# ReLU on VectorE, and forty gathered columns a turn in place of thirty-six

## The chip, the core and the metric

The kernel runs on one core of one Trainium2 chip. The core has TensorE (PE in the profile, its weight loads PEld), VectorE (DVE), ScalarE (ACT), GpSimd (POOL) and SyncE (SP). Each engine has an instruction queue of its own, worked off in order; rows of the profile marked with a q (DVEq, ACTq) are instructions that the queue's sequencer does itself, such as loading registers, and they don't count as busy. The metric is device time in microseconds of one execution, as the median of several runs. The span of a profile is the time from the first to the last instruction of one execution.

## The reference: what is computed

One layer of a graph network with 12,500 nodes of 64 features and 212,500 directed edges, sorted by their destination, with 32 features each:

```python
msg_in = jnp.concatenate([nodes[row], nodes[col], edge_features], axis=-1)
messages = _mlp(msg_in, mW1, mb1, mW2, mb2)      # relu(x @ W1 + b1) @ W2 + b2, hidden size 128
aggregated = jax.ops.segment_sum(messages, col, num_segments=nodes.shape[0])
upd_in = jnp.concatenate([nodes, aggregated], axis=-1)
return _mlp(upd_in, uW1, ub1, uW2, ub2)
# outside: x = _layernorm(x + this)
```

`row` is the source and `col` the destination of an edge. The source's features have to be fetched edge by edge, since sources are in no order; destinations come in order, so the edges of a stretch concern few neighbouring nodes.

## The kernel before, in words

Edges are worked on in groups of 384 (three tiles of 128); there are 554 groups, and the main loop of `ordered` (L718) has one turn for each. A turn of TensorE, written by `step` (L677), is three pieces of work for three different groups, with a single completion signal behind the last of them:

- `turn(k)` (L423): three transposes bring the gathered source features and a one-hot of the destinations (together 96 columns) of group k into PSUM (L429). ScalarE copies the result into the block `own_st` in SBUF (L440).
- `hidden(k - 2)` (L448): three matmuls with the weights `own_wm` (L453) give the hidden layer before the ReLU in PSUM. ScalarE makes the ReLU, 128x384, into `own_h` (L464).
- `sums(k - 4)` (L474): matmuls add the hidden rows by destination (L481) and count them (L486). VectorE adds both to the sums on the chip, at an address taken from a register (L495 and L496).

The next turn but one needs the same PSUM banks again, so TensorE may be one turn ahead of ScalarE and VectorE.

Source features arrive in one of two ways. For most groups GpSimd gathers rows of `x` from HBM by indirect DMA, three per group (L184), 16 groups ahead of the turn, into a ring of 20 buffers; a gather waits until the group 20 before has been copied out of its buffer and until that turn's copies on ScalarE are done (`marks_by`). For the groups listed in `COPIED` nothing is gathered: the transposed features of all nodes lie in SBUF (`own_xc`, 64 partitions by 12,500 nodes), and VectorE (L599) and ScalarE (L601) copy one column, 64 partitions by 4 bytes, per edge from there into `own_st`. `COLS` is how many columns are copied in each turn, from turn 18 (`BEGIN`) to turn 543. A group of 384 columns is listed as soon as the copies so far, `COLS` a turn, have filled it (L89 to L91); with `COLS` of 36 the list has 49 groups, the last of them 541. `VCOLS = (12, 8)` are VectorE's portions in a turn and `ACOLS = (16,)` ScalarE's.

A copy's source address comes from a register. `registers(k, part)` (L565) loads the addresses of one portion into registers of the engine (L578, TENSOR_LOAD on the engine's queue, as many registers as the portion has columns); `fetch(part)` (L585) issues the copies. The addresses themselves come by a DMA for eight turns at once (L557) and are scaled by one operation of VectorE (L563). `places` (L366, load at L371) loads four addresses for the additions, every fourth turn.

The order of VectorE's queue in a turn is: load of 12 addresses, two additions (L495, L496), 12 copies, the one-hot of a group six turns on (L412), load of 8 addresses, 8 copies. That the load of 12 stands ahead of the additions, which wait for TensorE, is the work of the list `between` (L738, popped at L493). ScalarE's queue in a turn is: copy of the transposed group (L440), ReLU (L464), 16 copies with addresses loaded in the turn before, load of 16 addresses for the next turn (L771).

Into the turns, pieces of `update` (L500) are placed: as soon as all edges of a chunk of nodes are done, its second layer and normalisation are computed, in six steps of one per turn (L528 and L543 among VectorE's operations). The last ten turns (`SHORT`) copy nothing and use shorter steps.

Of the kernel before, what the change touches and what calls it, by code (L numbers as in the profile page):

```python
# [14 lines left out]
AF = mybir.ActivationFunctionType  # L15
ALU = mybir.AluOpType
# [16 lines left out]
G = (E + GE - 1) // GE  # L33
# [17 lines left out]
BEGIN = 18  # L51
CHECKED = 8
VCOLS = (12, 8)
ACOLS = (16,)
COLS = sum(VCOLS + ACOLS)
SPAN = 8
STREAMS = ()
# [4 lines left out]
def tiles_of(g):  # L62

    n = min(GE, E - g * GE)
    return [min(P, n - j * P) for j in range((n + P - 1) // P)]
# [27 lines left out]
for _, rate, _ in STREAMS:  # L93
    BY_ROWS.append([])
    while True:
        last = BEGIN + (P * (len(BY_ROWS[-1]) + 1) - 1) // rate + ROW_LEAD
# [33 lines left out]
def ordered(ctx: ExitStack, tc: tile.TileContext, a, own, ok):  # L130
# [3 lines left out]
    nc = tc.nc  # L134
# [18 lines left out]
    loads, places_by, copy_by, relu_by, sums_by, wm_by, turn_by = ({} for _ in range(7))  # L153
# [5 lines left out]
    def after(first, *others):  # L159

        tc.declare_no_dep(first.ins, group="quiet", reason="waits for the last of a step")
        for i in others:
            tc.add_manual_dep(
                first.ins, i.ins.name,
                mybir.DependencyInfo(mybir.DependencyClass.Sync, mybir.DependencyReason.DATA),
                reason="the kernel's own rings",
            )
        return first
# [73 lines left out]
    def bit(k):  # L242

        nodes = [NEAR_NODES + (N - NEAR_NODES) * i // BITS for i in (k, k + 1)]
        tiles = [first + (NT - first) * i // BITS for i in (k, k + 1)]
        nc.sync.dma_start(src_sb[:, slice(*tiles)], a["src"][:, slice(*tiles)])
        nc.sync.dma_start(xc[:D, slice(*nodes)], a["xT"][:, slice(*nodes)])
        rest(nodes[0], nodes[1] if k < BITS - 1 else NP)

    def zeroed(k):  # L250

        n0, n1 = (NP * i // BITS for i in (k, k + 1))
        nc.vector.memset(agg[:, n0:n1], 0.0)
# [108 lines left out]
    def columns(g):  # L362
        t, c = own.st[g // SB % BLOCKS], (g % SB) * GE
        return t, c, sum(tiles_of(g))
# [83 lines left out]
    def hidden(g, ps):  # L448
        t, c, n = columns(g)
        sizes = tiles_of(g)  # L450
        pre = ps[1][:, : TG * H].rearrange("p (j h) -> p j h", h=H)
        did = [
            nc.tensor.matmul(pre[:p, j, :], t[:, c + j * P : c + j * P + p], wm[g % NW],  # L453
                             start=True, stop=True)
            for j, p in enumerate(sizes)
        ]
        needs = [*copy_by[g], *columns_by.get(g, {}).values(), wm_by[g], efs_by[g // SB],
                 *(wm_loads[g] if g < NW else ())]

        def relu(step):  # L460
            hidden_by[g] = step
            h = own.h[g % NH]
            if len(set(sizes)) == 1:
                relu_by[g] = [nc.scalar.activation(h, pre, AF.Relu)]  # L464
            else:
                relu_by[g] = [nc.scalar.activation(h[:p, j, :], pre[:p, j, :], AF.Relu)
                              for j, p in enumerate(sizes)]
            for i in relu_by[g]:
                after(i, step, *([sums_by[g - NH]] if g >= NH else []))
            return relu_by[g]  # L470

        return did, needs, relu

    def sums(g, ps):  # L474
        h, s = own.h[g % NH], own.s[g % RING]
        sizes = tiles_of(g)
        sg = ps[2][:, : TIMES * W].rearrange("p (t w) -> p t w", w=W)
        counted = ps[2][0:1, TIMES * W :][:, :W]
        did = []
        for j, p in enumerate(sizes):  # L480
            did.append(nc.tensor.matmul(  # L481
                sg, h[:p, j, :],
                s[:p, j, D:].unsqueeze(1).to_broadcast([p, TIMES, W]),
                start=j == 0, stop=j == len(sizes) - 1))
        for j, p in enumerate(sizes):
            did.append(nc.tensor.matmul(counted, own.one[:p], s[:p, j, D:],  # L486
                                        start=j == 0, stop=j == len(sizes) - 1))

        def add(step):
            sums_by[g] = step  # L490
            at = bass.ds(starts.pop(g), W)
            count = xc[COUNT : COUNT + 1, at]
            if between:  # L493
                between.pop()()
            a = after(nc.vector.tensor_tensor(agg[:, at], sg[:, 0, :], agg[:, at], ALU.add), step)  # L495
            return [a, after(nc.vector.tensor_tensor(count, counted, count, ALU.add), step)]  # L496

        return did, [*relu_by[g], *copy_by[g]], add
# [60 lines left out]
    def addresses(i):  # L559

        if i in indices:
            t = indices[i][:, : min(SPAN * COLS, GE * len(COPIED) - i * SPAN * COLS)]
            nc.vector.tensor_scalar(t, t, 4.0, float(own.at), ALU.mult, ALU.add)  # L563

    def registers(k, *parts):  # L565

        i, n = divmod(k - BEGIN, SPAN)
        if i < 0:
            return
        all_parts = [*((ET.DVE, c) for c in VCOLS), *((ET.Activation, c) for c in ACOLS)]  # L570
        for part in parts:
            engine, count = all_parts[part]
            c0 = (k - BEGIN) * COLS + sum(c for _, c in all_parts[:part])
            count = min(count, GE * len(COPIED) - c0)
            if count <= 0:
                return
            b = c0 - i * SPAN * COLS
            _, v = nc.values_load_multi_w_load_instructions(  # L578
                indices[i][0:1, b : b + count], engines=[engine],
                min_val=own.at, max_val=own.at + 4 * (N - 1),  # L580
                skip_runtime_bounds_check_because="a source is one of the nodes",
            )
            held[part] = engine, c0, v
# [42 lines left out]
    def row_addresses(n, i):  # L626

        if (n, i) in row_index:
            t = row_index[n, i][:, : row_span(n, i)[1]]
            nc.vector.tensor_scalar(t, t, 4.0 * D, None, ALU.mult)  # L630
# [82 lines left out]
    for n in range(len(STREAMS)):  # L713
        row_indexes(n, 0)
    made = summed = 0
    between, held, last = [], {}, {}

    for k in range(G):  # L718
        if k < BITS:
            bit(k)  # L720
            if k + 2 < BITS:
                zeroed(k + 2)
        if 1 < k < len(TABLE):
            projected(k)
        if k == CHECKED:
            addresses(0)
            for n in range(len(STREAMS)):
                row_addresses(n, 0)
            combined()
            ordered_edges()  # L730
            early.close()
            up = ctx.enter_context(tc.tile_pool(name="upd", bufs=2))
        if k % SB == 2:
            inputs(k // SB + 2)
        if k % SB == 1:
            places(k // SB + 1)
        if k < G - SHORT:
            between.append(lambda: registers(k, 0))  # L738
            step((turn, k), *([(hidden, k - 2)] if k > 1 else []),
                 *([(sums, k - 4)] if k > 3 else []))  # L740
            made, summed = max(0, k - 1), max(0, k - 3)
            if between:
                between.pop()()
        else:

            step((turn, k))
            for _ in range(2):
                if summed < made:
                    step((sums, summed))
                    summed += 1  # L750
            for _ in range(2):
                if made <= k:
                    step((hidden, made))
                    made += 1
            registers(k, 0)
        fetch(0)
        window(k + SB)
        for n in range(len(STREAMS)):
            row_numbers(n, k)
            row_fetch(n)  # L760
        onehot(k + LEAD)
        marks_by[k] = [copy_by[k][-1]]
        if k < G - 1:
            for part in range(1, len(VCOLS + ACOLS)):
                if part != len(VCOLS):
                    registers(k, part)
                fetch(part)
                if part >= len(VCOLS) and ET.Activation in last:
                    marks_by[k].append(last[ET.Activation])
            if k + 1 < G - 1:  # L770
                registers(k + 1, len(VCOLS))  # L771
            if k >= BEGIN and (k - BEGIN) % SPAN == 0:
                indexes((k - BEGIN) // SPAN + 1)
            if k >= BEGIN and (k - BEGIN) % SPAN == SPAN - 2:
                addresses((k - BEGIN) // SPAN + 1)
        if k + AHEAD < G:
            gather(k + AHEAD)
# [333 lines left out]
```

## Time and profile before

| | |
|---|---|
| median of three runs | 1913.65 us (1913.47 to 1916.86) |
| the profiled execution's own time | 1914.16 us |
| its span | 1912.4 us |
| mean granted TensorE clock | 0.972 |
| busy: GpSimd, ScalarE, TensorE, VectorE | 1431.7, 1325.2, 1324.3, 1251.4 us |
| gathers (L184) | 1514 |
| copied columns on VectorE (L599) and ScalarE (L601) | 10,460 and 8,356 |
| register loads on VectorE and ScalarE (L578) | 1,046 and 523 |

In a row of the list of groups, the numbers behind the bar are busy time in us (overlapping instructions counted once) and the mean duration of one in ns; behind the second bar stands the engine's idle time just before these instructions and what ended most of it. A row of waits has the total in us, how often, and the longest. A row of a stretch has its limits, its length, the busy time with the count of instructions that overlap the stretch, then the granted clock, the DMA share and GB/s. A row of time order has the start, the length, the instruction, and in brackets the idle time before it. A row of one source line has the minimum, median and maximum duration in ns, and the first and last start in us. Copies on one engine overlap each other, so that their mean duration is longer than the time from one to the next.

### The profile page before, as it was taken

The page shows a single profiled execution, that of the slowest core. Times are in us where ns is not written, and L with a number is a line of the kernel's source. Part 1 is how long each engine was busy: PE and PEld are TensorE (multiplying, and loading weights), DVE is VectorE, ACT ScalarE, POOL GpSimd, SP SyncE. Part 2 cuts the span into 40 slices and gives each one's busy share as a digit, 9 for nine tenths or more (in the row PEclk, how much of TensorE's full clock was granted, in tenths as well). Part 3 has the DMA queues.
Part 4 walks back from the last instruction along what each step waited for, and adds up shares of the span by engine and source line. Part 5 has one row for each costly group of instructions (what it writes and reads, how often), then busy time and mean ns, then how long its engine had stood idle before and what let it go on. Part 6 is the DMA issues. An engine that isn't in the chain of part 4 may idle for free. (4 is left out here: it accounts for less than half of the span.)

```text
span 1912.4 us, 56586 instructions
## 1 busy us (share of the span) xinstructions
PE 1324.3 (69%) x12323; PEld 1170.6 (61%) x12323; DVE 1251.4 (65%) x12584; ACT 1325.2 (69%) x9559; POOL 1431.7 (75%) x1521
## 2 busy tenths in 40 slices
PE   5877777767767766676666776766766766667677
PEld 4766666666656655665655665655656655556566
DVE  4347777766666666676766766666667666676662
ACT  4468787766767767776767776776676677676662
POOL 7777777777777777777777777777777777777774
PEclk9889999989999999999999999999999999999998
DMA  5532222222222222222222212222222222222221
GB/s 141 139 97 64 53 50 52 49 49 48 45 53 52 46 52 48 49 49 48 53 48 48 50 44 53 52 46 52 48 50 48 51 47 52 45 53 48 49 50 25
DMA packets 113836, 105.15 MB, mean 55 GB/s; under 512 B 52115, under 2 KB 83488, under 8 KB 113488
## 3 DMA queue, kind: packets, MB, share of 16 engines
q0 software_dynamic: 48448, 49.68, 13.6%
q1 hardware_dynamic: 64196, 51.29, 9.7%
q8 instruction: 104, 1.70, 0.4%
q14 instruction: 244, 2.00, 0.3%
q10 hardware_dynamic: 844, 0.48, 0.1%
HBM read 91.68 MB, written 9.62 MB: 53 GB/s over the span
## 5 line engine op out<-in xcount | busy, mean ns | idle before, releaser
L184 POOL DMA_INDIRECT own_s<-in_x,src_sb x1514 | 1430.9, 945 | 462.5 <-issue 261.5
L599 DVE COPY own_st<-own_xc 64x4 uint8 x10460 | 896.5, 191 | 27.7 <-DMA by_dst<-t 3.5
L601 ACT ACTIVATE own_st<-own_xc 64x4 uint8 x8356 | 847.3, 195 | 2.9 <-DMA by_dst<-t 2.9
L429 PE MATMUL own_ps<-own_ident,own_s 128*96 128x128 f32 x1661 | 289.0, 284 | 540.4 <-DMA own_s<-in_x,src_sb 355.6
L440 ACT ACTIVATE own_st<-own_ps 96x384 f32<-96x384 f32 (+1 forms) x554 | 268.6, 485 | 506.7 <-PE own_ps L486 483.7
L429 PEld LDWEIGHTS own_ps<-own_ident,own_s 128*96 128x96 f32 x1661 | 164.3, 129 | 602.0 <-ACT own_h L464 445.0
L481 PE MATMUL own_ps<-own_s,own_h 128*128 128x128 f32 x3322 | 478.6, 282 | 1.3 <-ACT own_h L464 0.6
L495 DVE TENSOR_TENSOR own_agg<-own_ps,own_agg 128x32 f32 x554 | 106.3, 192 | 567.1 <-PE own_ps L486 386.4
L453 PE MATMUL own_ps<-own_wm,own_st 128*128 128x128 f32 x3322 | 476.5, 281 | 0.0
L481 PEld LDWEIGHTS own_ps<-own_s,own_h 128*128 128x128 f32 x3322 | 431.1, 198 | 2.8 <-ACT own_h L464 1.6
L453 PEld LDWEIGHTS own_ps<-own_wm,own_st 128*128 128x128 f32 x3322 | 428.6, 197 | 1.3 <-issue 0.5
L464 ACT ACTIVATE own_h<-own_ps 128x384 f32<-128x384 f32 x553 | 264.8, 479 | 21.2 <-PE own_ps L453 20.0
L486 PE MATMUL own_ps<-own_s,own_one 128*1 128x32 f32 x3322 | 189.1, 194 | 0.0
L486 PEld LDWEIGHTS own_ps<-own_s,own_one 128*1 128x1 f32 x3322 | 113.8, 83 | 69.4 <-issue 5.7
L412 DVE TENSOR_TENSOR own_s<-iota,dlc 128x96 f32<-128x96 f32 x554 | 137.3, 248 | 0.7
L496 DVE TENSOR_TENSOR own_xc<-own_ps,own_xc 1x32 f32 x554 | 102.1, 184 | 31.9 <-PE u_ps L507 13.2
L383 PE MATMUL u_ps<-w1b,own_xc 65*128 65x128 f32 x196 | 31.8, 310 | 32.0 <-DMA own_xc<-in_xT 12.7
L383 PEld LDWEIGHTS u_ps<-w1b,own_xc 65*128 65x128 f32 x196 | 26.8, 211 | 35.0 <-issue 20.3
L519 PE MATMUL u_ps<-same,own_xc 65*128 65x64 f32 (+1 forms) x196 | 39.5, 283 | 0.4 <-ACT u L512 0.4
L386 ACT ACTIVATE t<-u_ps 128x512 f32<-128x512 f32 (+1 forms) x25 | 14.7, 588 | 36.2 <-DMA by_dst<-t 20.0
L521 PE MATMUL u_ps<-u,u 128*128 128x64 f32 (+1 forms) x196 | 38.2, 277 | 0.0
L519 PEld LDWEIGHTS u_ps<-same,own_xc 65*128 65x128 f32 (+1 forms) x196 | 29.9, 192 | 2.5 <-ACT u L512 1.0
(60 smaller groups left out, 264.4 us busy)
## 6 DMA issues: line engine op xcount, KB each, us to landing
own_st<-in_efT SPq DMA_DIRECT2D x138, 192.0 KB
own_s<-in_x,src_sb POOLq DMA_INDIRECT x1514
own_wm<-by_dst SPq DMA_DIRECT2D x554, 16.0 KB
by_dst<-t SPq DMA_DIRECT2D x24, 256.0 KB
out<-o SPq DMA_DIRECT2D x24, 128.0 KB
own_xc<-in_xT SPq DMA_DIRECT2D x12, 179.2 KB
index<-in_src_copied SPq DMA_DIRECT2D x65, 1.1 KB
dlc_i<-in_dst_cols SPq DMA_DIRECT2D x1, 807.0 KB
```

The lines of the kernel that those rows point to most:

```text
L184: nc.gpsimd.indirect_dma_start(out=s[:p, j, :D], out_offset=None, in_=x[:, :], in_offset=bass.IndirectOffsetOnAxis(ap=src_sb[:p, g * TG + ...
L412: places_by[g] = nc.vector.tensor_tensor(own.s[g % RING][:, :, D:], iota.unsqueeze(1).to_broadcast([P, TG, W]), dlc[:, g * TG : (g + 1) * ...
L429: nc.tensor.transpose(xt[:, j * P : j * P + p], sides[g] if g in sides and j == TG - 1 else s[:p, j, :], ident[:p, :p])
L440: after(nc.scalar.activation(t[r, c : c + n], xt[r, :n], AF.Copy), step))]
L453: nc.tensor.matmul(pre[:p, j, :], t[:, c + j * P : c + j * P + p], wm[g % NW], start=True, stop=True)
L464: relu_by[g] = [nc.scalar.activation(h, pre, AF.Relu)]
L481: did.append(nc.tensor.matmul(sg, h[:p, j, :], s[:p, j, D:].unsqueeze(1).to_broadcast([p, TIMES, W]), start=j == 0, stop=j == len(sizes) - 1))
L486: did.append(nc.tensor.matmul(counted, own.one[:p], s[:p, j, D:], start=j == 0, stop=j == len(sizes) - 1))
L495: a = after(nc.vector.tensor_tensor(agg[:, at], sg[:, 0, :], agg[:, at], ALU.add), step)
L496: return [a, after(nc.vector.tensor_tensor(count, counted, count, ALU.add), step)]
L599: by[engine] = nc.vector.tensor_copy(o, x_at)
L601: by[engine] = nc.scalar.activation(o, x_at, AF.Copy)
```

## The change

Three things are changed together. The ReLU of a group is made by VectorE (`tensor_scalar` with max against 0) and not by ScalarE. `ACOLS` is (8, 4, 4, 4) in place of (16,), so ScalarE copies 20 columns a turn, each portion loaded into registers just before its copies, and `COLS` is 40. And the list `between` is gone: VectorE's load of 12 addresses stands behind the ReLU and the two additions, and ScalarE's first load (8 addresses) stands behind L440 in the same turn, no longer at the end of the turn before.

```diff
-ACOLS = (16,)
+ACOLS = (8, 4, 4, 4)
...
             if len(set(sizes)) == 1:
-                relu_by[g] = [nc.scalar.activation(h, pre, AF.Relu)]
+                relu_by[g] = [nc.vector.tensor_scalar(h, pre, 0.0, None, ALU.max)]
             else:
-                relu_by[g] = [nc.scalar.activation(h[:p, j, :], pre[:p, j, :], AF.Relu)
+                relu_by[g] = [nc.vector.tensor_scalar(h[:p, j, :], pre[:p, j, :], 0.0, None, ALU.max)
                               for j, p in enumerate(sizes)]
...
             count = xc[COUNT : COUNT + 1, at]
-            if between:
-                between.pop()()
             a = after(nc.vector.tensor_tensor(agg[:, at], sg[:, 0, :], agg[:, at], ALU.add), step)
...
         if k < G - SHORT:
-            between.append(lambda: registers(k, 0))
             step((turn, k), *([(hidden, k - 2)] if k > 1 else []),
                  *([(sums, k - 4)] if k > 3 else []))
             made, summed = max(0, k - 1), max(0, k - 3)
-            if between:
-                between.pop()()
...
-            registers(k, 0)
+        registers(k, 0)
+        if k < G - 1:
+            registers(k, len(VCOLS))
         fetch(0)
...
-            if k + 1 < G - 1:
-                registers(k + 1, len(VCOLS))
```

More of the change, by code (lines that the diff above doesn't have):

```diff
@@ L715, in ordered @@
     made = summed = 0
-    between, held, last = [], {}, {}
+    held, last = {}, {}
     for k in range(G):
```

## The prediction

> **What bounds the kernel now.** I read the page first, then who waits for whom, then the turns counted by stretch, and last single turns of VectorE in order of time.
>
> ```profile
> span 1912.4 us, 56586 instructions
> PE 1324.3 (69%) x12323; PEld 1170.6 (61%) x12323; DVE 1251.4 (65%) x12584; ACT 1325.2 (69%) x9559; POOL 1431.7 (75%) x1521
> L184 POOL DMA_INDIRECT own_s<-in_x,src_sb x1514 | 1430.9, 945 | 462.5 <-issue 261.5
> POOL own_s L184 <- issue: 261.5, 858, 0.3
> POOL own_s L184 <- DMA own_s<-in_x,src_sb: 173.7, 570, 0.3
> 1894.07 0.90 POOL L184 DMA_INDIRECT own_s<-in_x,src_sb  x1 [0.30 <-DMA own_s<-in_x,src_sb]
> ```
>
> No engine is over 75% busy, yet GpSimd never rests. Each of its 1514 gathers has 0.945 us of work and a gap in front whose longest is 0.3 us, whatever the releaser is called: (1430.9 + 462.5) / 1514 = 1.251 us per gather. The last one ends at 1894.97, so 17.4 us of the span lie behind it. Gathers run from start to end without a stall; what they cost in total is the span but for about 19 us. The page's busy share hides this because the 0.3 us between gathers isn't counted.
>
> The other engines have slack, but not everywhere. ScalarE copies each turn's transposed features once (L440), so its count is the count of turns:
>
> ```profile
> 0.00:147.00 147.00, 14.51 (x30) 0.90 0.49 125
> 0.00:147.00 147.00, 109.33 (x114) 0.90 0.49 125
> 147.00:347.00 200.00, 32.48 (x67) 1.00 0.24 54
> 847.00:1347.00 500.00, 71.34 (x147) 0.98 0.22 49
> 1847.00:1912.40 65.40, 7.54 (x16) 0.91 0.15 32
> PE own_ps L429 <- ACT own_st L440: 19.9, 29, 1.5
> PE own_ps L429 <- DMA own_s<-in_x,src_sb: 113.5, 70, 2.2
> ```
>
> The second row counts gathers, the others L440. By 147 us there were 30 turns, but 114 gathers, which is 38 groups of three: GpSimd leads by some 9 groups. In the next 200 us turns come every 200 / 67 = 2.985 us; this is the pace of TensorE, VectorE and ScalarE when gathers lie ready (from 150 to 350 us TensorE's transposes wait for ScalarE, sixth row, and hardly for gathers). Once they have caught up, a turn takes 500 / 147 = 3.40 us and TensorE waits for gathers (last row, 847 to 1347 us). Between 147 and 1847 us there are 554 - 30 - 16 = 508 turns, 3.346 us each. So the kernel is bound by gathers, and the engines could do a turn in about 2.99.
>
> **What is removed.** A group whose 384 columns come from copies needs no gather. With COLS 36, 49 groups are copied; with 40 the same formula gives 54, the last being group 537. Gathers: 500 groups of three, less one in the short last group, 1499. That is 15 fewer: 15 x 1.251 = 18.8 us off GpSimd's stream. The 17.4 us behind the last gather stay, apart from the last ReLUs, which change engine (0.1 us). The profiled execution took 1914.16 (span 1912.4 and 1.8 around it), 0.5 above the median 1913.65. So 1914.2 - 18.8 = 1895.4, or 1895 beside the median, **if** the engines still fit under the gathers. With 18.8 less, 1700 us become 1681, and the 508 turns must average at most 3.31 us; at 3.346 nothing is gained. The question is by how much the pace of 2.985 grows.
>
> **VectorE.** It receives a ReLU of 128x384 from PSUM.
>
> ```profile
> L285 DVE TENSOR_SCALAR start_f<-own_ps x2: 423/424/425, 8.5 to 8.8; 1x277 f32<-1x277 f32 x2
> L495 DVE TENSOR_TENSOR own_agg<-own_ps,own_agg 128x32 f32 x554 | 106.3, 192 | 567.1 <-PE own_ps L486 386.4
> L464 ACT ACTIVATE own_h<-own_ps 128x384 f32<-128x384 f32 x553 | 264.8, 479 | 21.2 <-PE own_ps L453 20.0
> L599 DVE COPY own_st<-own_xc 64x4 uint8 x10460 | 896.5, 191 | 27.7 <-DMA by_dst<-t 3.5
> L578 DVEq TENSOR_LOAD <-index x1046: 592/844/1106, 88.7 to 1855.9; - x175
> ```
>
> The same operation on 277 elements from PSUM took 424 ns and an addition on 32 took 192: 0.95 ns an element, hence 424 + 107 x 0.95 = 0.53 us for 384 (bounds 0.42, as if length didn't matter, and 0.60). Some 0.07 of it overlaps the next instruction, as below with the one-hot. So 0.46 us of execution a turn. Whether it lengthens a turn depends on what a full turn of VectorE waits for:
>
> ```profile
> 1023.58 0.19 DVE L495 TENSOR_TENSOR own_agg<-own_ps,own_agg 128x32 f32 x1 [1.39 <-PE own_ps L486]
> 1023.80 0.18 DVE L496 TENSOR_TENSOR own_xc<-own_ps,own_xc 1x32 f32 x1
> 1024.02 0.94 DVE L599 COPY own_st<-own_xc 64x4 uint8 x12
> 1024.88 0.24 DVE L412 TENSOR_TENSOR own_s<-iota,dlc 128x96 f32<-128x96 f32 x1
> 1025.04 0.87 DVE L599 COPY own_st<-own_xc 64x4 uint8 x8
> 1026.29 0.19 DVE L495 TENSOR_TENSOR own_agg<-own_ps,own_agg 128x32 f32 x1 [0.37 <-DVE own_st L599]
> L578 DVEq TENSOR_LOAD <-index x1: 594/594/594, 1024.2 to 1024.2; - x1
> L578 DVEq TENSOR_LOAD <-index x1: 847/847/847, 1025.1 to 1025.1; - x1
> ```
>
> This turn takes 1026.29 - 1023.58 = 2.71 us. The last two rows are loads of registers in VectorE's instruction queue, not counted as busy. The load of 8 starts at 1024.2, while the twelve copies issued before it still run until 1024.9; so it overlaps execution. It ends at 1024.8, eight copies are issued in 0.3 us (0.04 each), the load of 12 runs from 1025.1 to 1026.0, and the additions follow 0.3 later. The queue sets the turn: 0.64 + 0.59 + 0.34 + 0.85 + 0.29 = 2.71. Execution alone needs 1025.04 - 1023.58 = 1.46 and eight copies at 896.5 / 10460 = 0.086, together 2.15.
>
> The change keeps both loads and moves that of 12 from ahead of the additions to behind them. To the queue it adds one issue, 0.04: 2.75. To execution it adds 0.46: 2.61, still less. But does a load run while instructions issued ahead of it execute, above all long ones? The turn of a finished chunk shows it:
>
> ```profile
> 449.34 1.10 DVE L543 TENSOR_SCALAR o<-u_ps,mv,rstd 128x64 f32<-128x64 f32 x4
> 450.43 0.19 DVE L495 TENSOR_TENSOR own_agg<-own_ps,own_agg 128x32 f32 x1
> L578 DVEq TENSOR_LOAD <-index x1: 851/851/851, 449.4 to 449.4; - x1
> ```
>
> Four operations on PSUM execute from 449.34 to 450.44, and the load of 12 behind them begins at 449.4. So in the changed kernel it should start some 0.4 us after the ReLU does (0.3 us of issue for the additions' addresses) and run behind ReLU and additions until 1.25. Twelve copies, the one-hot and eight copies end at about 1.35 + 12 x 0.086 + 0.17 + 0.69 = 3.2 us after the ReLU began. In a turn that waits for gathers (3 x 1.25 = 3.75) that is in time. In catching up, the next turn's issues overlap the last copies, and 2.75 is the pace. The price in the average is thus 0.04, with bounds of 0 and 0.65 (next part); I take 0.04 because the row at 449.4 is the same situation. What was hidden in the wait for TensorE (1.39 us in the first row) now lies behind it; its cover is the 3.75 us between gathers.
>
> **ScalarE.** It loses 0.479 of ReLU and gains four copies.
>
> ```profile
> L601 ACT ACTIVATE own_st<-own_xc 64x4 uint8 x8356 | 847.3, 195 | 2.9 <-DMA by_dst<-t 2.9
> L440 ACT ACTIVATE own_st<-own_ps 96x384 f32<-96x384 f32 (+1 forms) x554 | 268.6, 485 | 506.7 <-PE own_ps L486 483.7
> L578 ACTq TENSOR_LOAD <-index x523: 313/1021/1340, 90.2 to 1852.7; - x175
> L578 ACTq TENSOR_LOAD <-index x1: 313/313/313, 1852.7 to 1852.7; - x1
> ```
>
> Copies go at 847.3 / 8356 = 0.101 us, so execution is 0.485 + 20 x 0.101 = 2.51, against 0.485 + 0.479 + 1.62 = 2.58 now. Sixteen addresses load in 1.02 us; the last load of all, at 1852.7, is of the four columns left over, 0.313. That is 0.059 an address: the load of 8 about 0.55, the four loads together 0.55 + 3 x 0.313 = 1.49. With 21 issues of 0.04 and 0.09 behind each load the queue needs 2.7 us. The first load used to run at the end of the turn before; now it stands behind L440, which waits for TensorE, and the eight copies and all later ones are queued behind it: at most 0.55 us exposed. Each load of 4 lies behind copies still executing, as VectorE's load of 8 does. Those who wait for the last copy are the hidden layer of the copied group, turns later, and a gather 20 groups on, so neither is near. Bounds for ScalarE's turn: 2.51 with all hidden, 2.51 + 1.49 = 4.0 with nothing hidden; I take 2.7 to 2.8, which needn't exceed VectorE's.
>
> The Trainium skill speaks against small loads: "DMA: Bandwidth & Descriptors", section "Latency and other measured facts", gives a register load (tensor_load) a floor of about 600 ns. By that, ScalarE's four would take 2.4 us. The 0.313 above is under that floor, so I don't take it.
>
> **The sum.** Pace 2.985 + 0.04 = 3.03 us, well under 3.31. The lead of 9 groups (9 x 3.75 = 34 us) is worked off at 3.31 - 3.03 = 0.28 a turn in some 120 turns. Later, per 9.6 turns, one copied group makes the engines do two turns in one gather interval, after which they gain 0.7 in each. GpSimd stays the bound: 1895 us.
>
> **Rivals.** (a) Slower: the load of 12 isn't hidden behind ReLU and additions, but begins when they have executed. Then a full turn is 0.46 + 0.44, load 0.85, issue 0.1, twelve copies, one-hot and eight copies 1.7, less the overlaps: about 3.36 against 2.71, the 0.65 above. Pace 3.63; 508 x 3.63 + 147 + 65 + 2 = 2058 us. It decides from +0.33 a turn. For it: the additions need their own address computations. Against it: the load at 449.4. Chance 0.09.
>
> (b) Slower through ScalarE: a load of 4 costs nearly what the shortest full-sized load on VectorE costs, 0.592. Its queue then needs 4 x 0.59 + 4 x 0.09 + 21 x 0.04 = 3.56 a turn; 508 x 3.56 + 214 = 2022 us. By the skill's floor it would be the same. Against it stands one short load of 313 ns, alone at the end of the index row. Chance 0.05.
>
> (c) The engines take between 3.31 and 3.35 a turn, through the sum of updates, late additions and a throttled TensorE (0.98 of its clock from 847 to 1347 us): GpSimd gets ahead and the gain is eaten, 1905 to 1915 us. It needs eight times the price found. Chance 0.04.
>
> (d) The change doesn't remove the gathers' time, since each takes longer: 0.0125 us more on 1499 would do it, through a busier VectorE. Against it: the middle stretch has 377.86 / 401 = 0.942 us a gather, the first 109.33 / 114 = 0.959, though VectorE copies nothing in most of that.
>
> ```profile
> 847.00:1347.00 500.00, 377.86 (x401) 0.98 0.22 49
> ```
>
> Chance 0.02, 1914 us.
>
> **How the numbers follow.** The forecast, 1895 us, has 0.80; its own range is 1892 to 1899 (engines' jitter at the end, a gather more or less late). To hold more of (c) the upper end goes to 1907. A measurement of this kernel tells 0.2% (3.8 us) from no change. Faster 0.82 (forecast and part of c), same 0.04 (the rest of c, and d), slower 0.14 (a and b).
>
> **What would show it.** Right: 1499 gathers, still with 0.30 us in front of each; last gather's end near 1876; DVE's ReLU at 0.50 to 0.57 us; loads of 12 that start within 0.5 us of the ReLU; loads of 4 on ScalarE near 0.31; about 66 turns from 147 to 347 us; TensorE's longest waits still for gathers. Wrong: gaps on GpSimd above 0.3 us that a copy of ScalarE ends, full turns of VectorE above 3.3, or ScalarE's loads near 0.6.

## The result and the profile after

| | before | after |
|---|---|---|
| median of four runs | 1913.56 us | 1894.97 us (1894.76 to 1895.28) |
| the profiled execution: own time, span | 1914.16, 1912.4 us | 1894.96, 1893.1 us |
| gathers | 1514 | 1499 |
| copied columns, VectorE and ScalarE | 10,460 and 8,356 | 10,376 and 10,360 |

The ratio is 0.9899, with a 95% interval of 0.9882 to 0.9916: faster by 18.6 us. The forecast was 1895.

Ahead of each profile below stands what it is. First the page of the kernel after: span, busy times, and the groups of gathers, ScalarE's copies, VectorE's copies and the ReLU; then, from the answer on waits, GpSimd's and TensorE's longest, and the last gather in order of time.

```profile
span 1893.1 us, 60001 instructions
PE 1336.2 (71%) x12323; PEld 1182.5 (62%) x12323; DVE 1475.6 (78%) x13054; ACT 1385.6 (73%) x11008; POOL 1418.0 (75%) x1506
L184 POOL DMA_INDIRECT own_s<-in_x,src_sb x1499 | 1417.3, 945 | 457.9 <-DMA own_s<-in_x,src_sb 206.3
L599 ACT ACTIVATE own_st<-own_xc 64x4 uint8 x10360 | 1089.2, 191 | 66.7 <-issue 18.6
L597 DVE COPY own_st<-own_xc 64x4 uint8 x10376 | 894.5, 191 | 171.1 <-issue 146.9
L464 DVE TENSOR_SCALAR own_h<-own_ps 128x384 f32<-128x384 f32 x553 | 303.1, 548 | 167.4 <-PE own_ps L486 152.3
...
POOL own_s L184 <- DMA own_s<-in_x,src_sb: 206.3, 677, 0.3
POOL own_s L184 <- issue: 196.0, 643, 0.3
PE own_ps L429 <- ACT own_st L599: 230.9, 145, 2.2
PE own_ps L429 <- DMA own_s<-in_x,src_sb: 124.7, 88, 2.6
...
1875.89 0.89 POOL L184 DMA_INDIRECT own_s<-in_x,src_sb  x1 [0.30 <-issue]
```

VectorE is now the busiest by the page, 78% against GpSimd's 75%, and yet the gathers still set the time: (1417.3 + 457.9) / 1499 = 1.251 us each, as before, with gaps of 0.3 us, and the last ends at 1876.8, 18.2 us earlier than before. Behind it stand 16.3 us, 1.1 less than before. The share of busy time would have pointed at the wrong engine.

VectorE's turn, in order of time, from the kernel after, and the loads of registers in the same stretch (minimum, median and maximum duration, first and last start):

```profile
1006.38 0.56 DVE L464 TENSOR_SCALAR own_h<-own_ps 128x384 f32<-128x384 f32 x1
1006.86 0.18 DVE L493 TENSOR_TENSOR own_agg<-own_ps,own_agg 128x32 f32 x1
1007.07 0.18 DVE L494 TENSOR_TENSOR own_xc<-own_ps,own_xc 1x32 f32 x1
1007.66 0.99 DVE L597 COPY own_st<-own_xc 64x4 uint8 x12 [0.41 <-issue]
...
1009.32 0.54 DVE L464 TENSOR_SCALAR own_h<-own_ps 128x384 f32<-128x384 f32 x1
L576 DVEq TENSOR_LOAD <-index x1: 844/844/844, 1006.7 to 1006.7; - x1
```

The load of 12 starts at 1006.7, 0.3 us after the ReLU, and runs behind the ReLU and both additions. What isn't covered is the 0.41 us in front of the first copy. Over the run this gap comes 365 times and adds up to 146.9 us, the figure behind `issue` in the row of L597.

ScalarE's copies of the transposed groups, as a count of turns in two stretches of the kernel after, and the gathers in the second of them:

```profile
147.00:347.00 200.00, 32.15 (x67) 0.98 0.24 53
847.00:1347.00 500.00, 71.94 (x149) 0.96 0.22 50
847.00:1347.00 500.00, 378.09 (x401) 0.96 0.22 50
```

From 147 to 347 us, in most of which gathers lie ready, a turn takes 200 / 67 = 2.985 us, the same count as before. Once they don't, it takes 500 / 149 = 3.36 against 3.40 before: more groups are copied and fewer gathered, at the same rate of gathers (401 in 500 us in both).

### The profile page after: what moved, and what is told of

The parts are those of the page before. It is cut to its first block, busy times and chain, and to the rows that moved or that the text cites. A ratio compares the mean times of both kernels' runs of the same rounds, so it can differ in the third digit from the quotient of the medians.

```text
span 1893.1 us, 60001 instructions
## 1 busy us (share of the span) xinstructions
PE 1336.2 (71%) x12323; PEld 1182.5 (62%) x12323; DVE 1475.6 (78%) x13054; ACT 1385.6 (73%) x11008; POOL 1418.0 (75%) x1506
## 5 line engine op out<-in xcount | busy, mean ns | idle before, releaser
L184 POOL DMA_INDIRECT own_s<-in_x,src_sb x1499 | 1417.3, 945 | 457.9 <-DMA own_s<-in_x,src_sb 206.3
L599 ACT ACTIVATE own_st<-own_xc 64x4 uint8 x10360 | 1089.2, 191 | 66.7 <-issue 18.6
L597 DVE COPY own_st<-own_xc 64x4 uint8 x10376 | 894.5, 191 | 171.1 <-issue 146.9
L429 PE MATMUL own_ps<-own_ident,own_s 128*96 128x128 f32 x1661 | 292.4, 287 | 512.0 <-ACT own_st L599 230.9
L440 ACT ACTIVATE own_st<-own_ps 96x384 f32<-96x384 f32 (+1 forms) x554 | 267.3, 483 | 383.0 <-PE own_ps L486 341.6
L481 PE MATMUL own_ps<-own_s,own_h 128*128 128x128 f32 x3322 | 483.7, 284 | 1.9 <-DVE own_h L464 1.3
L481 PEld LDWEIGHTS own_ps<-own_s,own_h 128*128 128x128 f32 x3322 | 436.0, 200 | 3.8 <-DVE own_h L464 2.4
L464 DVE TENSOR_SCALAR own_h<-own_ps 128x384 f32<-128x384 f32 x553 | 303.1, 548 | 167.4 <-PE own_ps L486 152.3
L493 DVE TENSOR_TENSOR own_agg<-own_ps,own_agg 128x32 f32 x554 | 97.9, 177 | 18.1 <-PE own_ps L486 10.3
```

The lines of the kernel that those rows point to most:

```text
L184: nc.gpsimd.indirect_dma_start(out=s[:p, j, :D], out_offset=None, in_=x[:, :], in_offset=bass.IndirectOffsetOnAxis(ap=src_sb[:p, g * TG + ...
L429: nc.tensor.transpose(xt[:, j * P : j * P + p], sides[g] if g in sides and j == TG - 1 else s[:p, j, :], ident[:p, :p])
L440: after(nc.scalar.activation(t[r, c : c + n], xt[r, :n], AF.Copy), step))]
L464: relu_by[g] = [nc.vector.tensor_scalar(h, pre, 0.0, None, ALU.max)]
L481: did.append(nc.tensor.matmul(sg, h[:p, j, :], s[:p, j, D:].unsqueeze(1).to_broadcast([p, TIMES, W]), start=j == 0, stop=j == len(sizes) - 1))
L597: by[engine] = nc.vector.tensor_copy(o, x_at)
```

## Experiments

Twelve runs were made, of seven kernels, on several chips, and the chips differ. On two of them the kernel before takes 1913 to 1915 us, as in the result; on four it takes 2500 to 2540 us. Each ratio below is against the kernel before on the same chip. The first five runs were on chips of the second kind, so that the question was put again; the expectations of e1 to e4 were written for the first kind alone. The kernel after itself has no run on a chip of the second kind.

| run | kernel | before there | time | ratio (95% interval) |
|---|---|---|---|---|
| e6 | before, 15 gathers left out | 1914.56 | 1896.28 | 0.9901 (0.9882 to 0.9921) |
| e11 | after, ReLU on ScalarE | 1913.46 | 1894.60 | 0.9901 (0.9882 to 0.9921) |
| e1 | before, ReLU on VectorE | 2506.90 | 2521.45 | 1.0055 (1.0034 to 1.0076) |
| e2 | as e6 | 2506.90 | 2485.46 | 0.9931 (0.9904 to 0.9958) |
| e3, e7 | as e11 | 2506.90, 2502.33 | 2528.30, 2532.69 | 1.0086 (1.0058 to 1.0115), 1.0105 (1.0071 to 1.0138) |
| e4, e8 | after, load of 12 ahead | 2506.90, 2502.33 | 2542.05, 2536.64 | 1.0129 (1.0090 to 1.0169), 1.0124 (1.0087 to 1.0161) |
| e5, e9 | after, portions 8, 4, 4, 4, 4 | 2538.59, 2502.33 | 2579.33, 2538.81 | 1.0151 (1.0117 to 1.0186), 1.0137 (1.0098 to 1.0177) |
| e10 | after, ReLU twice | 2502.33 | 2588.86 | 1.0334 (1.0292 to 1.0376) |
| e12 | after, portions 8, 8, 8 | 2509.95 | 2536.77 | 1.0106 (1.0089 to 1.0123) |

**Fifteen gathers fewer, and nothing else (e2, e6).** The theory says that the gathers' stream sets the time, the rival that the change made the other engines faster. To tell them apart, the kernel before loses 15 gathers and keeps everything else; the middle third of 15 groups then holds old rows.

```diff
+LEFT_OUT = [g for g in range(100, 535) if g not in COPIED][::28][:15]
...
             if g not in columned and (j < TG - 1 or g not in sides)
+            and not (j == 1 and g in LEFT_OUT)
```

> The kernel before, but the middle one of three gathers is left out in 15 groups spread from group 100 to 492, so old rows stand in its place there. Nothing else changes. Theory: 1913.6 - 15 x 1.25 = 1894.9 us, within 2, the same as the whole change. Rival (the engines' pace bounds, and the change made them faster): within 3 us of 1913.6.

> The kernel before with the middle gather of 15 groups left out, once more, on whatever chip is given. If the kernel before takes about 1913 us there, gathers bound it and theory expects 1894.9 within 2; the rival (engines bound) expects 1911 to 1916. If the kernel before takes about 2500 us there, instructions arrive late, GpSimd waits for the other engines, and both expect little: within 1% of the kernel before.

On a chip of the first kind it took 1896.28 us, 18.3 less than the kernel before there: the whole gain, without any of the three changes. Page and order of time of e6:

```profile
span 1893.2 us, 56560 instructions
L185 POOL DMA_INDIRECT own_s<-in_x,src_sb x1499 | 1417.6, 946 | 457.8 <-issue 253.2
1876.10 0.90 POOL L185 DMA_INDIRECT own_s<-in_x,src_sb  x1 [0.30 <-issue]
```

Count, gap and end of the gathers are those of the kernel after, and so is the span to 0.1 us. The rival expected 1911 to 1916 and falls. On a chip of the second kind (e2) the same kernel gained 0.7%, 21.4 us; the expectation of e6, written later, says "within 1%" for such a chip.

**The ReLU back on ScalarE (e3, e7, e11).** Did the four additional columns need the move of the ReLU?

```diff
-                relu_by[g] = [nc.vector.tensor_scalar(h, pre, 0.0, None, ALU.max)]
+                relu_by[g] = [nc.scalar.activation(h, pre, AF.Relu)]
```

(and the same for the short last group).

> The changed kernel with the ReLU back on ScalarE: 40 columns a turn in 8, 4, 4, 4 and the new order of loads stay. ScalarE then executes 0.39 + 0.37 + 20 x 0.095 = 2.66 us a full turn, and its load of 8 lies behind copy and ReLU. Theory (gathers bound, pace under 3.31): 1895 us within 3, so the move of the ReLU wasn't needed. Rival (moving the ReLU is what made room for the four columns): ScalarE's turn over 3.31, 1900 to 1950 us.

> The changed kernel with the ReLU back on ScalarE; 40 columns a turn in 8, 4, 4, 4 and the new order of loads stay. Where the kernel before takes about 1913 us: ScalarE executes 0.39 + 0.37 + 20 x 0.095 = 2.66 us a full turn, its load of 8 behind copy and ReLU. Theory (gathers bound, pace under 3.31): 1895 us within 3, the move of the ReLU wasn't needed. Rival (moving the ReLU made the room for four more columns): ScalarE's turn over 3.31, 1900 to 1950 us. Where the kernel before takes about 2500 us: 0 to 2% slower than it.

> The changed kernel with the ReLU back on ScalarE, once more, on whatever chip is given; it has 1499 gathers. Where the kernel before takes about 1913 us: theory (gathers bound, ScalarE's full turn of 2.7 to 3.0 us fits under 3.31) 1895 us within 3; rival (moving the ReLU made the room for four more columns) 1900 to 1950 us. Where the kernel before takes about 2500 us: 1% slower than it, as twice already.

On a chip of the first kind: 1894.60 us, the kernel after's time. From the page of e11 the span and busy times, ScalarE's copies of groups in the stretch from 147 to 347 us, and VectorE's longest wait:

```profile
span 1893.0 us, 60470 instructions
PE 1334.8 (71%) x12323; PEld 1181.8 (62%) x12323; DVE 1236.6 (65%) x12499; ACT 1509.7 (80%) x11563; POOL 1418.4 (75%) x1506
...
147.00:347.00 200.00, 31.95 (x67) 0.99 0.23 54
...
DVE own_st L597 <- issue: 348.7, 554, 1.1
```

Where gathers bind, the ReLU costs nothing on either engine: the times agree to 0.4 us, and both kernels do 67 turns in these 200 us. ScalarE rises from 73% to 80% busy and still fits. The last row shows what the ReLU on VectorE does: without it the load of 12 leaves VectorE idle for 348.7 us in 554 gaps, 0.63 each; with it 146.9 in 365 gaps, 0.40 each. It fills idle time and lengthens nothing that can be measured here. The rival, that the move made room for the four columns, falls: the move wasn't needed for the gain. On the other chips (e3, e7) this kernel was 0.9 and 1.1% slower than the kernel before.

**The ReLU alone (e1).** The kernel before with the ReLU on VectorE.

> The kernel before with one part of the change: the ReLU on VectorE, portions and order of the loads as before. Theory (gathers bound, 1514 of them as before): 1913.6 us within 2, since the engines' pace may grow to 3.34 us a turn before it counts. Rival (the relief of ScalarE is what gained the time): most of the 18.6 us, under 1900. Rival (VectorE can't bear the ReLU): over 1918.

It ran on a chip of the second kind: 0.6% slower than the kernel before. There neither theory nor rivals apply, so this part alone, where gathers bind, wasn't measured. e11, with the reverse edit, answers for the kernel after.

**The load of 12 ahead of the ReLU (e4, e8).** One call of `registers(k, 0)` moves in front of `step`.

> The changed kernel with VectorE's load of 12 addresses put back ahead of the work that waits for TensorE, here ahead of the ReLU. Theory: in either place the load is hidden or fits under the gathers, 1895 us within 2. Rival (the order costs part of the gain, because the load behind the additions delays the copies): 1890 or less. Rival (ahead of the ReLU it delays the ReLU): over 1899.

> The changed kernel with VectorE's load of 12 addresses put back ahead of the work that waits for TensorE, here ahead of the ReLU. Where the kernel before takes about 1913 us: theory (in either place it is hidden or fits under the gathers) 1895 us within 2; rival (behind the additions it delays the copies and costs part of the gain) 1890 or less; rival (ahead of the ReLU it delays the ReLU) over 1899. Where the kernel before takes about 2500 us: 0 to 2% slower than it.

1.3 and 1.2% slower than the kernel before, on two chips of the second kind. What the order is worth where gathers bind stays open.

**Forty-four columns (e5, e9, e12).** `ACOLS = (8, 4, 4, 4, 4)`, and in e12 `(8, 8, 8)`.

> The changed kernel with one more portion of four on ScalarE: 44 columns a turn, 60 copied groups, 1481 gathers. Theory (gathers bound): 1913.6 - 33 x 1.25 = 1872.3 us within 3, if the engines' pace stays under (1700 - 41) / 508 = 3.27 us a turn; ScalarE executes 0.39 + 24 x 0.095 = 2.67 us a turn. Rival (engines already at the limit in the changed kernel): 1890 or more. On a chip where the kernel before itself takes much longer than 1913 us because instructions arrive late, gathers bound nothing and more instructions cost time: slower than the kernel before by 1 to 2%.

> The changed kernel with one more portion of four on ScalarE: 44 columns a turn, 60 copied groups, 1481 gathers. Where the kernel before takes about 1913 us: theory (gathers bound) 1913.6 - 33 x 1.25 = 1872.3 us within 3, if the engines' pace stays under (1700 - 41) / 508 = 3.27 us a turn, and ScalarE executes only 0.39 + 24 x 0.095 = 2.67; rival (engines at their limit already in the changed kernel) 1890 or more. Where the kernel before takes about 2500 us: 1 to 2% slower than it.

> The changed kernel with ScalarE's columns in three portions of eight: 44 columns a turn, 60 copied groups, 1481 gathers. ScalarE's queue: 3 x (0.55 load + 0.09 + 8 x 0.035 issue) = 2.8 us, execution 0.39 + 24 x 0.095 = 2.67. Where the kernel before takes about 1913 us: theory (gathers bound) 1913.6 - 33 x 1.25 = 1872.3 us within 3, if the engines' pace stays under (1700 - 41) / 508 = 3.27 us a turn; rival (engines at their limit already in the changed kernel) 1890 or more. Where the kernel before takes about 2500 us: 1 to 2% slower than it.

All three met chips of the second kind: 1.5, 1.4 and 1.1% slower than the kernel before, inside what was expected there. Whether 1481 gathers give 1872 us on the others wasn't measured; it is an expectation only.

**The ReLU twice (e10).** A second, equal `tensor_scalar` writes the same values again.

> The changed kernel with VectorE's ReLU made twice each turn (the second writes the same values again). VectorE's execution grows by 0.47 us, from 2.61 to 3.08 a full turn, and now exceeds its queue's 2.75. Theory (the first ReLU was hidden because the queue sets VectorE's turn): pace 2.99 + 3.08 - 2.75 = 3.3 us, at the limit of 3.31 under the gathers: 1895 to 1902 us. Rival (a ReLU on VectorE lengthens the turn by its whole execution, and the changed kernel is bound only just by gathers): pace 3.45, 147 + 508 x 3.45 + 66 = 1966 us. Where the kernel before takes about 2500 us: 1 to 4% slower than it.

3.3% slower than the kernel before, on the chip where e8 was 1.2% slower. The kernel after wasn't run there; if e8, which differs from it in one load's place, may stand for it, the second ReLU cost 52 us in 554 turns, 0.09 a turn for an instruction of 0.55 us, and even there most of it lay beside other work. Where gathers bind, it wasn't measured.

## Why the prediction was right, point by point

- **The bound.** The gathers' stream without a pause, 1.251 us each, was the bound. Shown: e6 takes 15 gathers away from the kernel before and gets the whole gain. 15 x 1.251 = 18.8 was put; 18.6 was measured for the change and 18.3 for e6. That 1895 and the measured 1894.97 agree so closely is luck: the last gather ends 18.2 us earlier and not 18.8, and the 17.4 us behind it, which were to stay, became 16.3. They did so in e6 too (1893.2 - 1877.0 = 16.2), so the move of the ReLU isn't the reason; what is stays open.
- **VectorE's ReLU.** 0.53 us was put (0.42 to 0.60); it takes 0.548.
- **The load of 12.** It was to start 0.4 us after the ReLU does and to run behind ReLU and additions; it starts 0.3 after. Rival (a), which had it begin when the additions have ended, falls by this row: the additions end at 1007.25, half a microsecond later. The turn is no exception: over the 494 turns of the trace with a ReLU, a load of 12 and all copies, the median start is 0.35 us after the ReLU's and 0.53 us before the additions end.
- **ScalarE's loads.** 0.313 was put for four addresses from a single row. Over all loads of the kernel after (minimum, median, maximum in ns):

```profile
L576 ACTq TENSOR_LOAD <-index x2072: 304/311/746, 95.0 to 1820.7; - x189
```

  Three in four of these are loads of four, and the median is 0.311. Rival (b) falls with that. The Trainium skill, "DMA: Bandwidth & Descriptors", section "Latency and other measured facts", gives such loads a floor of about 600 ns; the trace doesn't bear it out, and the measurement decides.
- **The pace of the engines.** 2.985 + 0.04 = 3.03 us a turn was put. The stretch from 147 to 347 us has 67 turns before and after, but such a count can't show 0.04: e6, whose engines do the work of the kernel before, has 65. And the lead of the gathers, to be worked off in some 120 turns, is gone after some 55 to 60: by the landings in the trace, nearly every wait in front of the transposes is for a gather from about 306 us on after and 325 before. So the end of the stretch goes at the gathers' pace already. The copies of the groups (L440, L442 in e6) from 147 to 300 us, in the kernel before, e6, the kernel after and e11:

```profile
L440 ACT ACTIVATE own_st<-own_ps x52: 466/486/487, 147.3 to 299.7; 96x384 f32<-96x384 f32 x48, 32x384 f32<-32x384 f32 x4
L442 ACT ACTIVATE own_st<-own_ps x50: 467/487/488, 150.0 to 296.8; 96x384 f32<-96x384 f32 x46, 32x384 f32<-32x384 f32 x4
L440 ACT ACTIVATE own_st<-own_ps x51: 466/486/488, 149.0 to 295.1; 96x384 f32<-96x384 f32 x46, 32x384 f32<-32x384 f32 x5
L440 ACT ACTIVATE own_st<-own_ps x52: 467/482/494, 148.1 to 298.7; 96x384 f32<-96x384 f32 x47, 32x384 f32<-32x384 f32 x5
```

  From first to last start that is 2.99 and 3.00 us a turn with the old portions and loads, 2.92 and 2.95 with the new. The 0.04 more can't be seen; a turn rather became a little shorter, whichever engine makes the ReLU, and why isn't shown. In any case the pace is far under the 3.31 that would have cost something, so rival (c) falls too. It also means that the argument on VectorE's queue, which took up most of the prediction, decided no more than that a limit wasn't reached.
- **Rival (d)**, slower gathers through a busier VectorE: 945 ns before and after, with VectorE at 65% and 78%.
- **One sign seems to fail, but holds.** TensorE's longest waits were to be for gathers still. By name they are for ScalarE's copies (L599), 230.9 us against 124.7. One such wait, in order of time, and the instructions of TensorE's queue (PEldq) ahead of it that wait for signals:

```profile
1105.43 0.94 POOL L184 DMA_INDIRECT own_s<-in_x,src_sb  x1 [0.30 <-issue]
1107.41 2.10 ACT L599 ACTIVATE own_st<-own_xc 64x4 uint8 x20 [0.15 <-issue]
1108.44 0.28 PEld L429 LDWEIGHTS own_ps<-own_ident,own_s 128*96 128x96 f32 x3 [1.84 <-ACT own_st L599]
L429 PEldq EVENT_SEMAPHORE  x3: 51/51/51, 1108.1 to 1108.4; - x3
```

  TensorE begins at 1108.44 while ScalarE's copies run until 1109.51, so it didn't wait for their end. In the trace's record of signals, the group's last gather, begun at 1105.43, lands at 1108.12; the first of the three queue instructions, which waits for it, runs right behind, and while the queue passes the other two a signal of ScalarE falls, at 1108.29, from the eighth copy. Its signals now stand behind the 8th, 12th and 20th copy, where the kernel before had one behind the 16th, and the profile names the last one to come. So it is over the run: from 306 to 1820 us TensorE waits 315 times by more than 0.35 us in front of the transposes, and 311 of these waits end within 0.6 us of the landing of the group's last gather.

What isn't settled for the kernel after: whether the new order of the loads matters (e4 and e8 met other chips), and how far one may go with the columns.

## What to carry to other kernels

An engine can be the bound at 75% busy, below another's 78%: look for the one whose gaps never exceed a constant, and multiply its period by the count of its instructions. Moving work to an engine that becomes the busiest by it costs nothing while the slack under such a stream lasts, so work out that slack (here 3.31 us a turn against 2.99) before costing the move itself, and prove the bound by taking some of the stream's work away and nothing else. Measure on more than one chip: the same kernel that gained 1% where the stream ran unbroken (e11) lost 1% where it didn't (e3, e7).

## What the runs showed that was not expected

The same kernel took 1896.28 us on one chip (e6) and 2485.46 on another (e2). From e2, copies of VectorE and of ScalarE in order of time, the longest wait of ScalarE and one of GpSimd, the groups of gathers and of ScalarE's copies, and VectorE's loads of registers; below, in a fence of its own, ScalarE's copies on the chip of e6.

```profile
1309.85 0.17 DVE L601 COPY own_st<-own_xc 64x4 uint8 x1 [0.41 <-issue]
1310.56 0.16 DVE L601 COPY own_st<-own_xc 64x4 uint8 x1 [0.54 <-issue]
1311.28 0.17 DVE L601 COPY own_st<-own_xc 64x4 uint8 x1 [0.56 <-issue]
...
1309.85 0.21 ACT L603 ACTIVATE own_st<-own_xc 64x4 uint8 x1 [0.51 <-issue]
1310.55 0.20 ACT L603 ACTIVATE own_st<-own_xc 64x4 uint8 x1 [0.50 <-issue]
1311.27 0.20 ACT L603 ACTIVATE own_st<-own_xc 64x4 uint8 x1 [0.52 <-issue]
...
ACT own_st L442 <- remote: 499.9, 140, 24.7
POOL own_s L185 <- ACT own_st L442: 299.7, 132, 11.8
...
L185 POOL DMA_INDIRECT own_s<-in_x,src_sb x1499 | 1417.3, 945 | 998.5 <-issue 341.6
L603 ACT ACTIVATE own_st<-own_xc 64x4 uint8 x8356 | 889.8, 195 | 215.7 <-issue 212.9
L580 DVEq TENSOR_LOAD <-index x1046: 593/843/971, 167.7 to 2435.8; - x175
```

```profile
L603 ACT ACTIVATE own_st<-own_xc 64x4 uint8 x8356 | 847.2, 195 | 2.6 <-DMA own_xc<-in_xT 2.6
```

Copies of one portion, whose addresses are loaded and which wait for nothing, come 0.7 us apart on both engines at the same times, where 0.07 and 0.10 is usual. On ScalarE that idle time is 215.7 us against 2.6. The copies themselves, the gathers and the loads of registers last as long as ever. It looks as if both queues were given their instructions one at a time, which the expectations of e5 and e6 call instructions that arrive late; that is an inference, since the profile shows no cause ("issue" is time in which an engine waited for nothing that the profile shows, and `remote` a wait whose releaser it didn't find). GpSimd waits for ScalarE there, up to 11.8 us at a time, and is idle for 998.5 us in front of its gathers where e6 has 457.8, so the gathers don't run as one unbroken stream. That they cost nothing there doesn't follow, since 15 fewer gained 21.4 us in e2; how is open. Kernels with more instructions lose: 60,001 or 60,470 against 56,586 cost 0.9 to 1.3%, 61,766 cost 1.1%, 62,812 cost 1.4 and 1.5%. The count alone doesn't explain it, since e10 with 60,546 loses 3.3% and e1, with fewer than the kernel before, 0.6%. The granted TensorE clock was lower as well, 0.827 in e2 against 0.968 in e6; whether as cause or consequence, these runs don't tell. Nor do they tell what sets the two kinds of chips apart.
